# Small products of an attention adapter in 32-column weights, four column groups side by side

## The chip, the cores and the metric

The kernel runs on one core of a Trainium2 chip. The metric is the device time of one execution in microseconds; of several executions the median is taken. TensorE (PE in the profile) multiplies, VectorE (DVE) and ScalarE (ACT) compute element by element and empty PSUM, GpSimd (POOL) fills constants, scales and issues indirect transfers, and SyncE (SP) issues the other transfers.

## The reference

Everything is float32. x is 2 x 2048 x 640, the context 2 x 128 x 384; its last four rows of each batch belong to an adapter. There are eight heads of 80 columns.

```python
enc, ca = context[:, :124], context[:, 124:]
hs      = mha(x @ Wq, enc @ Wk, enc @ Wv)             # 8 heads
ca_q1   = einsum('btc,th->bch', ca, Wq_ca)            # 384 rows
ca_q1   = ca_q1[:, linspace(0, 383, 2048)]            # each row used several times
ca_hs1  = mha(ca_q1, x, x)
ca_hs2  = mha(ca_hs1 @ Wq, ca @ Wk_ca, ca @ Wv_ca)    # 4 keys per head
out     = (hs + ca_hs2) @ Wout + b_out + x
```

## The kernel before, in words

The adapter's first attention has only 384 different query rows, so it is computed for 384 rows and repeated at the end by an indirect transfer that adds rows to the result. Its second attention has four keys a head. A softmax over four scores needs only differences, so three differences of keys a head are enough. The kernel multiplies these differences with Wq ahead of time and gets, for each batch, a small matrix of 24 columns (8 heads x 3). This matrix and Wq_ca stand side by side in the tiles `wyz` and `wyz4`. Multiplied with a block of x (512 rows) they give `yz`: scores of the adapter on one side, and what its values are contracted with on the other. The values of the adapter are likewise multiplied with Wout ahead of time into `w2_sb`.

The edited parts are these.

- `setup_a2` (L437). It multiplies ca with Wk_ca into the PSUM tile `p2_kca` (in the profile `p_kca`): five chunks of 128 columns of Wk_ca are the weights, three parts of the contraction each, and eight columns of context (2 batches x 4 rows) are the moving side. DVE takes differences and multiplies them with a mask of heads, which gives `blk_kca`, 48 columns. Then for each of five chunks i of Wq's rows, Wq is transposed on TensorE (`pt_wq`, five transposes), copied by ACT (`wqT`), and five products with `blk_kca` as the moving side go to the PSUM tile `pa`. `spread_yz` (L422) writes `pa` into `wyz` and `wyz4`, eight DVE steps.
- `setup_values` (L540). It issues the loads of Wout, multiplies ca with Wv_ca (`pvca`: weights of 8 columns, 320 moving columns, six products), transposes that (`pt_vca`), copies it, masks it on DVE (`blk_vca`, 64 columns), computes the values of the text (`pv`, `vpad`), and multiplies `blk_vca` with Wout (`pw`: weights of 64 columns, 320 moving columns, ten products) into `w2_sb`.
- `contraction` (L776). Near its end it writes the probabilities of the second adapter attention into `p2pad`, 65 columns (64 and one of ones for the bias), transposes it and multiplies it with `w2_sb` (the profile shows these as `po<-w_sb,p2T`).

All products pass through one helper, so they carry line L28; transposes carry L41, DVE's steps L55, most copies L268, and SP's transfers L247.

**What sets the order of the work.** TensorE's instructions stay in the order in which the program writes them. That order is made by a planner. `weave` (L1106) runs a main sequence that yields a number of microseconds at certain points; at each, so many microseconds of filling work are written, by a running estimate `pe.us` of TensorE's time. There are two fills: `own` (setup of keys and values, loads and turnings of x, the yz blocks, in this order) and `text` (the queries of the text, block by block). The fill that has used less time goes first; a part that waits for an earlier one is passed over. `fill.until` forces one part to its end without the other fill. In setup the main sequence is `setup_a2`, then the yz block of x block 0, then `maxima` (L743), which for each x block multiplies six times four row groups into a PSUM tile of four banks (`s`), reduced by DVE in one step (`mx`, 128x2048).

A block of x comes by eight transfers on SP (`x_load`, L675, tile `xi`, one buffer) and is turned by five DVE transposes (`x_turn`, L694, tile `xt`). A turning is written when 24 us of `pe.us` have passed since its load; where no data order forbids it, the order of DVE's instructions is settled when the program is built, from estimated times, so it can differ from the written one. The next load waits until the buffer `xi` is free, and the transfers on SP keep their written order: the loads of Wout stand behind the load of x block 3. PSUM tiles of the setup come from a pool of three (`ps_m`) and one of a single tile (`ps_a`).

Of the kernel before, what the change touches and what calls it, by code (L numbers as in the profile page):

```python
# [8 lines left out]
F32 = mybir.dt.float32  # L9
# [4 lines left out]
P = 128  # L14
HEADS = 8
# [158 lines left out]
def kernel(  # L174
# [114 lines left out]

# [36 lines left out]
    N2 = B * HEADS * T  # L326
    w2_sb = const.tile([N2 + 1, H], F32, name="w2_sb")
    p2pad = const.tile([P, NCC, N2 + 1], F32, name="p2pad")
# [66 lines left out]
    caT = sp.tile([P, NCC, B * T], F32, name="caT")  # L395
    wqcaT = sp.tile([P, NCH, T], F32, name="wqcaT")

    def setup_first():

        for cc in range(NCC):  # L400
            pt = mm_tile(f"pt_ctx_{cc}")
            for b in range(B):
                transpose(
                    pt[:, b * NTOK : (b + 1) * NTOK], ctx_sb[:, b, cc * P : (cc + 1) * P], ident
                )
            evacuate(ctxT[:, cc, :, :].rearrange("p b t -> p (b t)"), pt[:, : B * NTOK])
        dve.tensor_copy(
            caT.rearrange("p c (b t) -> p c b t", b=B), ctxT[:, :, :, NK:]
        )
# [26 lines left out]

    def setup_a2():  # L437

        mask = sp.tile([P, NCH, HEADS], F32, tag="mask", name="mask")
        nc.gpsimd.memset(mask, 0.0)  # L440
        for c in range(4):
            nc.gpsimd.tensor_copy(mask[:, c, 2 * c : 2 * c + 2], side)
        nc.gpsimd.tensor_copy(mask[:, 4, :].rearrange("p (g j) -> p g j", j=2)[:, :, 1], quarter)
        kca_of = columns(w_c["kca"], sp.tile([P, NCC, P], F32, tag="w4", name="kca4"))
        p2 = mm_tile("p2_kca")
        for c in range(NCH):
            for cc in range(NCC):
                matmul(
                    p2[:, c * B * T : (c + 1) * B * T],
                    kca_of(cc, c),  # L450
                    caT[:, cc, :],
                    start=(cc == 0),
                    stop=(cc == NCC - 1),
                )
        yield 4.0
        load_w("vca", Wv_ca)
        flat = sp.tile([P, NCH, B, T], F32, name="flat_kca")
        dve.tensor_copy(flat.rearrange("p c b t -> p (c b t)"), p2[:, : NCH * B * T])
        diff = sp.tile([P, NCH, B, T1], F32, name="diff_kca")
        dve.tensor_tensor(  # L460
            diff, flat[:, :, :, 1:], flat[:, :, :, :1].to_broadcast([P, NCH, B, T1]), ALU.subtract
        )
        blk = sp.tile([P, NCH, B, HEADS, T1], F32, tag="blk", name="blk_kca")
        for b in range(B):
            dve.tensor_tensor(
                blk[:, :, b, :, :],
                diff[:, :, b, :].unsqueeze(2).to_broadcast([P, NCH, HEADS, T1]),
                mask.unsqueeze(3).to_broadcast([P, NCH, HEADS, T1]),
                ALU.mult,
            )  # L470

        pa = mm_tile("pa2", ps_a)
        for i in range(NCH):
            wqT = sp.tile([P, NCH, P], F32, tag="wqT", name=f"wqT_{i}", bufs=2)
            for c0, c1 in ((0, 4), (4, NCH)):
                pt = mm_tile(f"pt_wq_{i}_{c0}")
                for c in range(c0, c1):
                    transpose(
                        pt[:, (c - c0) * P : (c - c0 + 1) * P],
                        wq_of(i, c),  # L480
                        ident,
                    )
                evacuate(
                    wqT[:, c0:c1, :].rearrange("p c s -> p (c s)"), pt[:, : (c1 - c0) * P]
                )
            yield 1.5
            for c in range(NCH):
                matmul(
                    pa[:, i * B * Y : (i + 1) * B * Y],
                    wqT[:, c, :],  # L490
                    blk[:, c, :, :, :].rearrange("p b h t -> p (b h t)"),
                    start=(c == 0),
                    stop=(c == NCH - 1),
                )
            yield 1.5
        spread_yz(pa[:, : NCH * B * Y].rearrange("p (i b k) -> p i b k", i=NCH, b=B), 0)
# [43 lines left out]
    def setup_values():  # L540
# [10 lines left out]
        vca = sp.tile([B * T, NCH * P], F32, name="vca")  # L551

# [13 lines left out]
        for u in range(2):  # L566
            pv = mm_tile(f"pvca_{u}")
            for cc in range(NCC):
                matmul(
                    pv[: B * T, :HALF],  # L570
                    caT[:, cc, :],
                    w_c["vca"][:, cc, u * HALF : (u + 1) * HALF],
                    start=(cc == 0),
                    stop=(cc == NCC - 1),
                )
            s4 = pv[: B * T, :HALF].rearrange("p (h d) -> p h d", h=4)
            evacuate(
                vca[:, : 4 * P].rearrange("p (h d) -> p h d", d=VH)[:, 4 * u : 4 * u + 4],
                s4[:, :, :VH],
            )  # L580
            evacuate(
                vca[:, 4 * P :].rearrange("p (h d) -> p h d", d=VR)[:, 4 * u : 4 * u + 4],
                s4[:, :, VH:],
            )
            yield
        pt = mm_tile("pt_vca")
        for c in range(NCH):
            transpose(
                pt[:, c * B * T : (c + 1) * B * T], vca[:, c * P : (c + 1) * P],
                ident[: B * T, : B * T],  # L590
            )
        vcaT = sp.tile([P, NCH, B, T], F32, name="vcaT")
        evacuate(vcaT.rearrange("p c b t -> p (c b t)"), pt[:, : NCH * B * T])
        mask = sp.tile([P, NCH, HEADS], F32, tag="mask", name="mask_v")
        nc.gpsimd.memset(mask, 0.0)
        for c in range(4):
            nc.gpsimd.tensor_copy(mask[:, c, 2 * c : 2 * c + 2], side2)
        nc.gpsimd.tensor_copy(mask[:, 4, :], eighth)
        blk = sp.tile([P, NCH, B, HEADS, T], F32, tag="blk", name="blk_vca")
        for b in range(B):  # L600
            dve.tensor_tensor(
                blk[:, :, b, :, :],
                vcaT[:, :, b, :].unsqueeze(2).to_broadcast([P, NCH, HEADS, T]),
                mask.unsqueeze(3).to_broadcast([P, NCH, HEADS, T]),
                ALU.mult,
            )
        yield
        for b in range(B):
            nc.gpsimd.memset(vpad[b], 0.0)
            for u in range(2):  # L610
# [10 lines left out]
                yield  # L621
        for u in range(2):
            pw = mm_tile(f"pw2_{u}")
            for c in range(NCH):
                matmul(
                    pw[:N2, :HALF],
                    blk[:, c, :, :, :].rearrange("p b h t -> p (b h t)"),
                    wout_sb[:, c, u * HALF : (u + 1) * HALF],
                    start=(c == 0), stop=(c == NCH - 1),
                )  # L630
            evacuate(w2_sb[:N2, u * HALF : (u + 1) * HALF], pw[:N2, :HALF])
            yield
# [143 lines left out]
    def contraction(b, sq, gap):  # L776
# [4 lines left out]
        nc.gpsimd.memset(p2pad[:, :, N2:], 1.0)  # L781
# [63 lines left out]
        n2 = b * HEADS * T  # L845
        dve.tensor_tensor(
# [411 lines left out]
```

## Time and profile before

| what | us |
|---|---|
| median of 3 runs | 773.32 |
| lowest, highest | 772.04, 779.84 |
| profiled execution, whole | 769.24 |
| its span in the profile | 767.5 |
| TensorE busy in the span | 740.0 |
| DVE busy | 374.5 |
| first to last of setup_a2's own products (p_kca to pa) | 22.7 to 51.3 |
| values' setup (pvca to pw) | 99.6 to 117.2 |

The span runs from the first to the last instruction of the profiled execution; 1.7 us of its time lie outside. A product of float32 appears as two instructions, called passes here. A group such as `128*32 128x384` has weights of 128 rows and 32 columns and 384 moving columns. The chain of waits is followed back from the last instruction, at each step to what released it. Ends of TensorE's instructions are modelled, so the distance from one group's start to the next one's is the better measure of what it takes.

### The profile page before, as it was taken

How to read it: one execution, taken by the hardware profiler on the slowest of the kernel's cores; microseconds unless marked ns; L12 is line 12 of the kernel's file. 1: busy time of each engine (PE TensorE's matmuls, PEld its weight loads, DVE VectorE, ACT ScalarE, POOL GpSimd, SP SyncE). 2: the span in 40 equal slices, each digit the busy share in tenths (PEclk: the TensorE clock that was granted, in tenths of full speed). 3: DMA queues.
4: the chain of work that ended last, by engine and by line, in shares of the span. 5: the costliest groups of instructions: out<-in, count | busy, mean ns of one | idle time of the engine just before them, and what ended most of it. 6: DMA issues, size and time to landing. Idle time of an engine off the chain costs nothing.

```text
span 767.5 us, 9354 instructions
## 1 busy us (share of the span) xinstructions
PE 740.0 (96%) x3785; PEld 379.0 (49%) x3785; DVE 374.5 (49%) x502; ACT 195.0 (25%) x241; POOL 134.3 (17%) x192
## 2 busy tenths in 40 slices
PE   7989999999998999989999999999999999999997
PEld 4653343343354445555545454444533556556664
DVE  2134753562365345478758586421530626346631
ACT  2212121104344433231111110443534321011100
POOL 7000000000111012217221221010010023432320
PEclk9999999999999999999999999999999999999999
DMA  9705530000476674499997277320920427785873
GB/s 288 164 2 67 77 79 0 1 0 1 140 122 139 149 123 130 134 255 178 261 189 205 53 153 128 115 48 18 185 63 1 152 69 228 159 218 165 220 213 91
DMA packets 146853, 95.63 MB, mean 125 GB/s; under 512 B 118069, under 2 KB 118389, under 8 KB 144762
## 3 DMA queue, kind: packets, MB, share of 16 engines
q1 hardware_dynamic: 141690, 84.44, 44.8%
q0 software_dynamic: 5120, 10.59, 8.0%
q8 instruction: 30, 0.49, 0.3%
q14 instruction: 13, 0.11, 0.1%
HBM read 63.48 MB, written 31.52 MB: 124 GB/s over the span
## 4 chain that ended last, share of the span: by engine, by line
PE 87%; DVE 6%; DMA 2%; ACT 2%; issue 2%; SPq 0%; POOL 0%; DVEq 0%; ACTq 0%; POOLq 0%
PE po L28 22%; PE pq L28 22%; PE s L28 13%; PE sc L28 10%; PE acc L28 6%; PE ph L28 5%; PE pyz L28 3%; DVE m L55 1%; PE pk L28 1%; DVE p L55 1%; ACT ea L807 1%; PE pt_y L41 1%; DVE mx L55 1%; PE pv L28 1%; DMA pT<-kept 1%
## 5 line engine op out<-in xcount | busy, mean ns | idle before, releaser
L28 PE MATMUL po<-wout_sb,hsT 128*128 128x320 f32 x640 | 187.4, 438 | 0.9 <-DVE xo L55 0.6
L28 PEld LDWEIGHTS po<-wout_sb,hsT 128*128 128x128 f32 x640 | 118.3, 190 | 72.0 <-issue 28.2
L55 DVE TENSOR_REDUCE mx<-s 128x4 f32<-128x2048 f32 x48 | 109.9, 2289 | 83.1 <-PE s L28 83.0
L28 PE MATMUL pq<-xt,wq_sb 128*128 128x512 f32 x320 | 150.2, 605 | 0.0
L807 ACT ACTIVATE ea<-s 128x1536 f32<-128x1536 f32 x64 | 92.7, 1448 | 105.3 <-PE s L28 105.1
L55 DVE TENSOR_TENSOR xo<-xo,po 128x320 f32<-128x320 f32 x64 | 30.9, 483 | 152.7 <-PE po L28 152.7
L962 POOL TENSOR_TENSOR p<-p,r 128x992 f32<-128x992 f32 x32 | 63.6, 2030 | 231.2 <-DVE r L55 231.2
L28 PE MATMUL sc<-kpad,q 128*128 128x248 f32 x384 | 95.4, 385 | 2.2 <-DVE p L55 1.6
L28 PEld LDWEIGHTS pq<-xt,wq_sb 128*128 128x128 f32 x320 | 57.4, 189 | 79.4 <-issue 74.7
L28 PEld LDWEIGHTS sc<-kpad,q 128*128 128x128 f32 x384 | 68.8, 189 | 32.9 <-issue 19.5
L28 PE MATMUL s<-ca,yz 32*128 32x384 f32 x512 | 59.4, 533 | 4.5 <-ACT ea L807 4.1
L268 ACT COPY q<-pq 128x512 f32<-128x512 f32 x30 | 17.6, 585 | 164.2 <-PE pq L28 164.2
L55 DVE TENSOR_REDUCE m<-sc 128x4 f32<-128x496 f32 x64 | 42.2, 662 | 34.0 <-PE sc L28 34.0
L28 PE MATMUL s<-yz,ca 32*128 32x512 f32 x384 | 54.7, 640 | 3.2 <-DVE mx L55 3.2
L1044 POOL DMA_INDIRECT xo<-o,query x25 | 39.2, 1569 | 92.5 <-DVE xo L55 24.1
L28 PE MATMUL acc<-ea,y_sb 128*32 128x384 f32 x512 | 54.6, 498 | 0.0
L28 PE MATMUL ph<-pT,vpad 128*32 128x256 f32 (+1 forms) x512 | 51.1, 387 | 2.1 <-DMA pT<-kept 1.9
L947 ACT ACTIVATE p<-p 128x992 f32<-128x992 f32 x32 | 33.0, 1030 | 74.2 <-DVE p L55 73.9
L55 DVE TENSOR_TENSOR p<-sc,m 128x496 f32<-128x496 f32 x64 | 42.6, 668 | 1.6
L268 ACT COPY hsT<-ph 128x512 f32<-128x512 f32 (+1 forms) x25 | 12.9, 515 | 106.2 <-PE ph L28 106.2
L55 DVE STREAM_TRANSPOSE eb<-p 128x1024 f32<-128x1024 f32 x32 | 38.0, 1221 | 2.2 <-POOL p L962 2.2
L55 DVE TENSOR_REDUCE r<-p 128x8 f32<-128x992 f32 (+1 forms) x34 | 37.9, 1115 | 0.0
(136 smaller groups left out, 435.5 us busy)
## 6 DMA issues: line engine op xcount, KB each, us to landing
kept<-eb SPq DMA_DIRECT2D x16, 1024.0 KB, 4.8
pT<-kept SPq DMA_DIRECT2D x64, 256.0 KB, 5.2
xi<-in_x_dram SPq DMA_DIRECT2D x44, 256.0 KB, 5.9
xo<-in_x_dram SPq DMA_DIRECT2D x32, 320.0 KB, 5.0
out_dram<-xo SPq DMA_DIRECT2D x25, 320.0 KB, 2.6
xi<-in_x_dram SPq DMA_DIRECT2D x44, 64.0 KB, 5.0
early<-xo SPq DMA_DIRECT2D x7, 320.0 KB, 2.2
xe<-early SPq DMA_DIRECT2D x7, 320.0 KB, 5.1
```

What stands on the lines that cost most here:

```text
L28: ins = self.tc.nc.tensor.matmul(out, lhsT, rhs, **kw)
L41: ins = self.tc.nc.tensor.transpose(out, in_, ident)
L55: self.last = getattr(self.tc.nc.vector, name)(*args, **kw).ins
L268: nc.scalar.copy(dst, src)
L807: nc.scalar.activation(e, q4[:, :, :CAD], AF.Exp, scale=SCALE)
L947: nc.scalar.activation(e[:, :, :NK], e[:, :, :NK], AF.Exp, scale=SCALE)
L962: nc.gpsimd.tensor_tensor(et, et, r.unsqueeze(2).to_broadcast([P, HEADS, NK]), ALU.mult)
L1044: nc.gpsimd.indirect_dma_start(out=t, out_offset=None, in_=o2_of[b], in_offset=bass.IndirectOffsetOnAxis(ap=query[:, st : st + 1], axis=0) ...
```

## The change

Four things are turned round.

- **ca with Wk_ca and Wv_ca** (`by_groups`): the rows of context are now the weights (32 columns, of which 6 or 8 are used; the differences of keys are taken beforehand, in `cadT`), and the columns of Wk_ca or Wv_ca move, 160 at a time. Four pairs of heads go to the four groups of 32 partitions of one PSUM tile. Twelve products take the place of 15 (keys) and 6 (values).
- **The turned form** (`groups_turned`): one transpose of 128 columns, and four small products with the identity for the remaining 32 columns of each pair of heads.
- **With Wq and Wout** (`by_blocks`): the masked blocks `blk` are the weights, 32 columns per pair of heads in four column groups, and then one product with all 128 columns for the chunk of remaining columns. Wq's transposes and the rows of Wout move (128 and 320 columns). With Wq the result is turned, so it is copied to `a2`, transposed five times and spread by eight DVE steps (`spread_chunks`). All five `wqT` are now kept until the end and multiplied in one go.
- **The layout of w2_sb and p2pad**: four groups of 32 instead of 64 columns in a row, so the last contraction has 113 rows instead of 65, and `p2pad` is written by two DVE steps instead of one.

The yields of `setup_a2` change with it: before 4.0 and ten of 1.5, now 2.0 and seven of 1.5. The small matrices of zeros are filled by POOL at the start.

```diff
-    N2 = B * HEADS * T
+    N2 = 3 * G + 2 * B * T
...
-    p2pad = const.tile([P, NCC, N2 + 1], F32, name="p2pad")
+    p2pad = const.tile([P, NCC, P], F32, name="p2pad")
...
+    for t in (caT, cadT, blk["k"], blk["v"]):
+        nc.gpsimd.memset(t, 0.0)
...
+    def by_groups(name, rows, w):
+        pg = mm_tile(name)
+        for cc in range(NCC):
+            for g in range(4):
+                matmul(
+                    pg[G * g : G * (g + 1), :D2], rows[:, cc, :], w[:, cc, D2 * g : D2 * (g + 1)],
+                    start=(cc == 0), stop=(cc == NCC - 1), skip_group_check=True,
+                )
+        return pg
+
+    def groups_turned(name, t, n):
+        pt = mm_tile(name)
+        transpose(pt[:, :P], t[:, :P], ident)
+        for g in range(4):
+            matmul(
+                pt[R * g : R * (g + 1), P : P + n], t[:, P:], ident[:, G * g : G * g + n],
+                start=True, stop=True, skip_group_check=True,
+            )
+        return pt[:, :P].rearrange("p (c k) -> p c k", c=4), pt[:, P : P + n]
+
+    def by_blocks(name, *products):
+        for to, rhs, first in products:
+            for c in range(4):
+                matmul(
+                    to[G * c : G * (c + 1)], blk[name][:, 0, c, :], rhs(c),
+                    start=first, stop=False, skip_group_check=True,
+                )
+        for to, rhs, _ in products:
+            matmul(
+                to, blk[name][:, 1].rearrange("p g k -> p (g k)"), rhs(4),
+                start=False, stop=True, skip_group_check=True,
+            )
...
     def setup_a2():
+        pg = by_groups("p2_kca", cadT, w_c["kca"])
+        k2 = sp.tile([P, D2], F32, name="k2")
+        evacuate(k2, pg[:, :D2])
+        yield 2.0
         load_w("vca", Wv_ca)
...
             yield 1.5
-            for c in range(NCH):
-                matmul(
-                    pa[:, i * B * Y : (i + 1) * B * Y],
-                    wqT[:, c, :],
-                    blk[:, c, :, :, :].rearrange("p b h t -> p (b h t)"),
...
+            if i == 0:
+                most, rest = groups_turned("pt_k2", k2, B * T1)
...
+                yield 1.5
+        a2 = sp.tile([P, NCH * P], F32, name="a2")
+        pa = [mm_tile("pa2_0", ps_a), mm_tile("pa2_1")]
+        by_blocks(
+            "k",
+            *[(pa[i // 4][:, i % 4 * P : (i % 4 + 1) * P], lambda c, t=wqT[i]: t[:, c], i % 4 == 0)
+              for i in range(NCH)],
+        )
+        nc.scalar.copy(a2[:, : 4 * P], pa[0])
+        dve.tensor_copy(a2[:, 4 * P :], pa[1][:, :P])
+        yield 1.5
+        for c0, c1 in ((0, 4), (4, NCH)):
+            pt = mm_tile(f"pt_a2_{c0}")
+            for c in range(c0, c1):
+                transpose(pt[:, (c - c0) * P : (c - c0 + 1) * P], a2[:, c * P : (c + 1) * P], ident)
+            for b in range(B):
+                n = 2 * T1
+                w = pt[:, : (c1 - c0) * P].rearrange("p (c g k) -> p c g k", g=4, k=G)
+                spread_chunks(w[:, :, :, n * b : n * (b + 1)], b, c0)
...
+        pg = by_groups("pvca", caT, w_c["vca"])[:, :D2].rearrange("p (j d) -> p j d", j=2)
...
+        most, rest = groups_turned("pt_vca", vca, B * T)
...
+        yield
         for u in range(2):
-            pw = mm_tile(f"pw2_{u}")
...
+            cols = slice(u * HALF, (u + 1) * HALF)
+            pw = mm_tile(f"pw2_{u}")[:, :HALF]
+            by_blocks("v", (pw, lambda c: wout_sb[:, c, cols], True))
+            evacuate(w2_sb[:N2, cols], pw[:N2])
+        yield
...
-        dve.tensor_tensor(
-            p2pad[:, :, n2 : n2 + HEADS * T].rearrange("p a (h t) -> p a h t", t=T), p2.rearrange("p (a h) t -> p a h t", a=NCC),
...
+        for j in range(2):
+            k0 = 2 * T * b + T * j
+            dve.tensor_tensor(
+                p2pad[:, :, : 4 * G].rearrange("p a (g k) -> p a g k", g=4)[:, :, :, k0 : k0 + T],
...
```

## The prediction

> **What bounds the kernel now.** I read the page first (busy shares, slices, chain of waits), then the chain in order of time and the windows for the first 170 us, where all the edited code but one step runs, then the timeline for the nearest rows of the new operations.
>
> ```profile
> PE 740.0 (96%) x3785; PEld 379.0 (49%) x3785; DVE 374.5 (49%) x502; ACT 195.0 (25%) x241; POOL 134.3 (17%) x192
> PE 87%; DVE 6%; DMA 2%; ACT 2%; issue 2%; SPq 0%; POOL 0%; DVEq 0%; ACTq 0%; POOLq 0%
> ```
> These are the page's busy line and the chain's shares: TensorE is the path, so an instruction taken from it is worth its own pitch, provided that nothing else then comes late. The chain in order of time shows what the edited products cost:
>
> ```profile
> 22.70 3.25 PE p_kca L28 x30
> ...
> 49.38 0.59 ACT wqT L268
> ...
> 50.02 1.33 PE pa L28 x10
> ...
> 52.22 4.55 PE pyz L28 x12
> ...
> 72.38 2.93 PE pyz L28 x12
> ...
> 99.59 3.34 PE pvca L28 x12
> ...
> 103.72 1.81 PE pv L28 x6
> ...
> 111.65 5.26 PE pw L28 x19
> ```
> Columns are start, length, engine and tile. A float32 product appears as two passes (x30 for 15 products). The first pyz takes 4.55 us, the next, equal one 2.93. The windows say why, in the column before the last two (granted clock, 1.00 and 0.80):
>
> ```profile
> 22.70:51.34 28.64, 27.38 (x155) 20.77 (x154) 6.20 (x17) 5.43 (x13) 0.81 (x6) 1.00 0.39 96
> 51.34:59.80 8.46, 6.82 (x29) 2.38 (x29) 4.58 (x13) 2.43 (x4) 0.00 (x0) 0.80 0.30 47
> ```
>
> **Price of a 32-column pass.** The timeline has two such groups, four column groups side by side, each with the start of its successor:
>
> ```profile
> 177.00 0.85 PE L28 MATMUL acc<-ea,y_sb 128*32 128x384 f32 x8
> 177.79 1.98 PE L28 MATMUL pq<-xt,wq_sb 128*128 128x512 f32 x4
> 304.51 1.07 PE L28 MATMUL ph<-pT,vpad 128*32 128x256 f32 x16
> 305.51 1.52 PE L28 MATMUL sc<-kpad,q 128*128 128x248 f32 x6
> ```
> Ten full-width po passes of 320 columns take 2.69 us in the chain, 0.84 ns a column. acc needs 0.79 us for two sets of four passes: 2 x 384 x 0.84 = 0.645, leaving 0.14. ph needs 1.00 for four sets: 4 x 256 x 0.84 = 0.86, leaving 0.14. So four passes cost as much as one, plus about 0.14 us a block. [...]
>
> **Setup of the adapter's keys (setup_a2).** Removed: p_kca 3.25; pa, four times 1.05 and once 1.33, 5.5. Together 8.8. Its stalls: 0.6 before the last pa (waits for ACT's wqT), 0.9 before pyz (waits for DVE's wyz), 1.6 for the half clock (4.55 - 2.93).
> Added on TensorE:
> - by_groups, 12 products of 160 columns = 6 sets. Lower end 6 x 160 x 0.84 = 0.8; upper end, if a set can't be shorter than the shortest seen (ph's 0.215), 1.3; with 0.14 I take 1.2.
> - groups_turned: one transpose 0.11 (pt rows) and eight tiny passes, between 0.2 (side by side) and 0.7 (one by one at pt_vca's 0.09); with 0.14, 0.6.
> - by_blocks: 20 narrow products of 128 columns = 10 sets, 1.1 to 2.15, and five full ones, 10 passes x 0.11 = 1.1: 2.8 with the block.
> - five transposes of a2, 0.55.
>
> Sum 5.15 against 8.8. The copies of a2 (ACT 0.59 by the 128x512 wqT row, DVE about 0.2) lie behind two pq products (1.7 us) that the planner's 1.5 lets in; uncovered they would cost 0.7. The spread's eight DVE steps lie behind the last pq product (0.86) but for 0.3. With the fill shorter, pk steps follow each other with only 0.55 us of transposes between, while DVE needs 2 x 0.43 to empty one and three PSUM buffers turn: twice 0.4, against 0.34 today, so +0.5. I expect full clock at pyz, as wide products stand in each stretch ahead of it.
>
> **Setup of the values.** Removed: 99.59 to 103.72 (pvca, its transposes and their wait for ACT) 4.1, and pw 5.3. Added: by_groups 1.2, groups_turned 0.6, by_blocks twice 2 sets x 320 x 0.84 + 2 passes x 0.27 + 0.14 = 2 x 1.2 = 2.4. Here a wait is added: the four DVE steps that build blk stand between the turned groups and by_blocks, and the planner is then forcing this stage alone to reach the next yz block, so no pq fills in. Four steps at 0.23 to 0.28 (pitches of the wyz and blk_vca rows) and the way through PSUM: 1.25. All of TensorE's queue stands behind it, as it keeps program order.
>
> **Elsewhere.** p2pad is written by two DVE steps instead of one. In the second contraction TensorE already waits 0.58 for it, and the one step took 0.91 there (0.25 in the first): +0.3, at most 0.9. The transposes stay at 128 moving columns and the products on w2 at 320; 113 rows instead of 65 in the contraction cost nothing: four passes of 320 columns take 1.24 us with 65 rows (po on w_sb) as with 128 (po on wout_sb). The four memsets on POOL (wyz's 128x256 took 0.30, s2f's 128x96 0.17: 0.9 in all) go ahead of 22 us, and POOL is idle for 12 us from 14.8 on; caT's copy on DVE may wait for them, 1 us at most, and is needed at 22.7. No DMA is added; SP's order stays.
>
> **Sum.** Removed 18.2 of products and 3.1 of stalls. Added 5.15 + 4.2 = 9.35 of products (ends about 8 and 11.3) and waits of 0.5 + 0.3 + 1.25 + 0.3 = 2.35. Saved 9.6 us: of the profiled execution's 769.24 (span 767.5) that makes 759.6; of the median 773.32, four above it, 763.7. I say 764. From 170 us on the instruction stream on TensorE is the same, and it is the path there, so I take the lead as kept.
>
> **Rivals.**
> A: the turning of x block 1 falls behind a reduction. Today DVE does those five transposes at 52.88, in its idle time before the first maximum:
>
> ```profile
> 52.88 3.07 DVE L55 STREAM_TRANSPOSE xt<-xi 128x512 f32<-128x512 f32 x5
> 59.94 2.29 DVE L55 TENSOR_REDUCE mx<-s 128x4 f32<-128x2048 f32 x1 [3.99 <-PE s L28]
> ```
> They stand after that maximum in the program and were placed ahead of it by an order fixed at build time. Their data had long landed, and DVE's idle time before 51 was not used, so the order reckoned with a later landing. With TensorE some 8 us ahead, the first scores come at about 50 us, and the maximum (2.3), perhaps the last kpad steps (1.6), go first; the queries of block 1 then wait 4 to 5 us. [...] Saved then 9.6 - 5 - 0.8 = 3.8, so 769.5. For it: the placement of the second block's turn, split around a maximum. Against: the order depends on reckoned times that no row shows.
> B: the column groups don't run side by side for these short passes. Then by_groups costs 24 x 0.134 = 3.2 twice, the k blocks 4.4 + 1.1, the v blocks 5.3, with the rest 19 us against 18.2 removed: 773. The acc and ph rows speak against it.
> C, slower: the weights for pw come late. The Wout loads are queued on SP behind the load of x block 3, which waits until block 2 is turned (84.7); they end at about 105. With the products ahead of pw shorter by 3 us, the slack of 6 shrinks to 3. If block 2's turn slips behind further maxima (3.8 us a step), by_blocks waits with all of TensorE behind it. Together with A's 5.8 this turns the sign once Wout is over 3.8 us late, that is, after a slip of 7, two steps: 775 to 783.
>
> **How the numbers follow.** The main case 50%, A 32%, B 8%, C 10%. A measurement of this kernel tells about 1% from no change (its runs span 772 to 780). 1% is 7.7 us: the main case (763.7, 3 to either side) passes it three times in four, A one in six, so faster 0.43, slower by over 1% only in C's far half, 0.06. The range: 759 (all costs at their lower ends, 1.4 less, and some of the noise) to 773 (A and B).
>
> **What would show it.** In the profile after: p_kca and pvca as 128*32 groups of about 1 us; by_blocks on pa and pw 2.8 and twice 1.2; pyz the first time at 2.9 with clock 1.00; the first maximum starting near 51 us instead of 59.9, and pq right behind the first scores (main) or after an idle stretch of 4 us ended by DVE's xt (A); a wait of about 1.2 before pw on DVE's blk; sc of the first tile near 158 instead of 168. The prediction is wrong if the 32-column passes have a floor above 0.05 us each, if the clock falls elsewhere, or if the order on DVE shifts after 170 us and gives the lead back.

## The result and the profile after

The changed kernel takes 762.52 us (median of six executions, 759.39 to 765.65) against 774.19 of the kernel before (six, 772.04 to 779.84). The ratio on record is 0.9859 with a 95% interval of 0.9825 to 0.9892 (the quotient of these two medians is 0.985): faster, by more than 1%. Predicted were 764.0 us in a range of 759 to 773. The profiled execution after is 764.96 us (span 763.3). It belongs to the slower half of the six: three took 759.4 to 760.3 us, three 764.7 to 765.7.

The page's busy line and the chain's shares of the kernel after:

```profile
PE 734.3 (96%) x3809; PEld 372.8 (49%) x3809; DVE 374.9 (49%) x506; ACT 195.3 (26%) x240; POOL 133.7 (18%) x184
PE 87%; DVE 6%; DMA 3%; ACT 2%; issue 1%; POOL 0%; SPq 0%; DVEq 0%; ACTq 0%; POOLq 0%
```

TensorE is still the path. The chain of waits in order of time (start, length, engine and tile), after:

```profile
9.08 2.29 DVE x_last L55
...
13.57 14.56 PE pq L28 x30
28.13 0.95 PE p_kca L28 x24
...
45.56 2.54 PE pa L28 x50
...
51.43 3.05 PE pyz L28 x12
...
99.19 0.95 PE pvca L28 x24
...
109.00 2.89 PE pw L28 x20
```

The keys' first products fell from 3.25 to 0.95 us, those of `pvca` from 3.34 to 0.95, `pw` from 5.26 to 2.89, and the first `pyz` from 4.55 to 3.05. But the edited stage starts later: `p_kca` at 28.1 us, where it stood at 22.7 (22.54 by the start of its first pass, which the next table uses). The windows of the same two stretches as before show the clock (the column before the last two) at 1.00 in both:

```profile
28.06:51.43 23.37, 22.03 (x158) 14.33 (x158) 5.35 (x18) 5.89 (x15) 0.00 (x0) 1.00 0.38 101
51.43:59.80 8.37, 7.59 (x37) 3.71 (x38) 5.60 (x10) 2.84 (x5) 0.00 (x0) 1.00 0.46 67
```

Cut into stages by the starts of TensorE's groups, the two profiled executions compare so (us):

| stage | before | after | difference |
|---|---|---|---|
| start to the first p_kca | 22.54 | 28.06 | +5.52 |
| p_kca to the first scores s | 36.11 | 28.31 | -7.80 |
| s to the first sc of the text | 109.33 | 106.48 | -2.85 |
| first sc to the end | 599.57 | 600.41 | +0.84 |
| span | 767.55 | 763.26 | -4.29 |

The cut at the first s does not part equal work. The last group of pk takes 1.40 us (46.22 to 47.62 before, 57.44 to 58.84 after, start to start); it stood ahead of the first scores and now stands behind them. For equal work the two differences are -6.40 and -4.25.

The edited stretch, from p_kca to the first sc, gives 10.65 us, and more than half of it is lost again before that stretch begins. These are the two things that the experiments have to explain. "Stage" below means p_kca to the first sc, 145.44 us before and 134.79 after.

### The profile page after: what moved, and what is told of

Read it like the earlier page. It is cut to its first block, busy times and chain, and to the rows that moved or that the text cites. A ratio compares the mean times of both kernels' runs of the same rounds, so it can differ in the third digit from the quotient of the medians.

```text
span 763.3 us, 9394 instructions
## 1 busy us (share of the span) xinstructions
PE 734.3 (96%) x3809; PEld 372.8 (49%) x3809; DVE 374.9 (49%) x506; ACT 195.3 (26%) x240; POOL 133.7 (18%) x184
## 4 chain that ended last, share of the span: by engine, by line
PE 87%; DVE 6%; DMA 3%; ACT 2%; issue 1%; POOL 0%; SPq 0%; DVEq 0%; ACTq 0%; POOLq 0%
PE po L28 22%; PE pq L28 22%; PE s L28 13%; PE sc L28 10%; PE acc L28 6%; PE ph L28 6%; PE pyz L28 3%; PE pk L28 1%; ACT ea L846 1%; PE pt_y L41 1%; DVE mx L55 1%; DMA pT<-kept 1%; PE pv L28 1%; DVE p L55 1%; DVE m L55 1%
## 5 line engine op out<-in xcount | busy, mean ns | idle before, releaser
L28 PE MATMUL pq<-xt,wq 128*128 128x512 f32 x80 | 38.0, 603 | 0.0
```

Source lines behind the costliest of these rows:

```text
L28: ins = self.tc.nc.tensor.matmul(out, lhsT, rhs, **kw)
```

## Experiments

### Each half alone

The first kernel keeps the keys' edits and has the values as before, the second the reverse (both diffs against the kernel after).

```diff
-        pg = by_groups("pvca", caT, w_c["vca"])[:, :D2].rearrange("p (j d) -> p j d", j=2)
...
+        for u in range(2):
+            pv = mm_tile(f"pvca_{u}")
...
```

```diff
-        pg = by_groups("p2_kca", cadT, w_c["kca"])
...
+        p2 = mm_tile("p2_kca")
...
```

> The keys' products turned round as in the change; the values' products, w2_sb and p2pad as before. My theory (TensorE is the path, each part gives what it takes from it): the stretch from the start of p_kca to the end of the first pk of the last chunk falls from 37.1 us to about 30.9, and the rest is as before: 6 us faster than the kernel before. Rival (the gain is that of the values alone, or the keys' gain is only the half clock at the first pyz that happened to go): about 1.6 us faster, with the stretch at 35.5.

> The values' products, w2_sb and p2pad turned round; the keys' products as before. My theory: the stretch from there to the first sc falls from 108.2 us to about 103.9, the first stretch stays at 37.1 with the half clock at the first pyz (length 4.5), so 4 to 4.5 us faster than the kernel before; together with the keys alone the sum of the change. Rival (the wait on the four DVE steps and the broader contraction give it back): no difference.

Keys alone took 764.84 us (ratio 0.9894, 0.9852 to 0.9935), with a stage of 139.42 us: 6.02 less than before. It is 7.82 less up to the first s and 1.80 more behind it: 1.40 is the group of pk that now stands there, and TensorE waits longer for the maxima. Total, number and longest of these waits, before and then in this kernel:

```profile
PE s L28 <- DVE mx L55: 3.2, 3, 1.4
PE s L28 <- DVE mx L55: 3.7, 4, 1.4
```

The kernel after has the second line too. Values alone took 767.41 (0.9917, 0.9897 to 0.9937). There the stretch that holds the values, s to the first sc, is 104.79 us, 4.54 less; p_kca to s grew by 2.87, for this execution ran 3.41 us from 26.66 and 6.83 from 53.96 at half clock, where the profiled one of before had 3.41 from 51.89. The halves add up: 6.02 + 4.54 = 10.56, against 10.65 for both. The medians lie further under the 774.02 of the kernel before in the same session (9.2 and 6.6 us), but they hold the start and the clock as well; the stages are the measure of the edits.

### Group after group

The 24 passes of each by_groups go out with all contraction parts of one column group before the next group, instead of the four groups in turn. It was to test rival B: what the passes cost when they do not run side by side.

```diff
-        for cc in range(NCC):
-            for g in range(4):
+        for g in range(4):
+            for cc in range(NCC):
                 matmul(
                     pg[G * g : G * (g + 1), :D2], rows[:, cc, :], ...
```

> The change, but by_groups takes the three parts of one column group one after another, and only then the next group; same 12 products each. My theory (four neighbouring products in four column groups run side by side, and products of one group follow each other): p_kca and pvca take about 24 x 0.134 = 3.2 us each instead of 0.95, so 4.5 us slower than the change. Rival (what counts is the 32-column weight, or the queue finds the side-by-side order itself): 0.95 each, no difference to the change.

762.48 us (0.9839, 0.9809 to 0.9869); the stage is 136.55 us, 1.76 more than after, or 0.88 for each by_groups. TensorE's timeline shows the first of them, ahead of pk, at 31.29 - 29.45 = 1.84 us:

```profile
29.45 1.91 PE L28 MATMUL p_kca<-w_kca,cadT 128*32 128x160 f32 x24
31.29 1.56 PE L28 MATMUL pk<-ctxT,w_k 128*128 128x256 f32 x6
```

The single passes explain it. In the kernel after, the four passes of a set start 7 ns apart, and the sets 136 (the first 160). Here passes of one group start 136 ns apart, but the next group's first pass starts about 0.30 us after the first pass of the group ahead, while that one still runs. So TensorE overlapped the groups here, 0.30 us apart, though the program has them one after another, and this order never gave the serial case; the 3.2 us for each group, which rival B and the expectation had, did not appear even here, and the order of the program is worth 0.88 us for each.

### Block 1 turned behind the first maximum

Rival A as an experiment: DVE's order is held so that the five transposes of x block 1 come after the first maximum.

```diff
+            elif behind_max:
+                dve.behind(ins, behind_max.pop())
...
+                if (b, sb, ct, u) == (0, 0, 0, 0):
+                    behind_max.append(dve.last)
```

> The change, with the turning of x block 1 kept behind the first maximum on DVE. This is rival A of the prediction, made to happen. If its price was sized rightly: after the first scores and the last pk, TensorE is idle 4 to 5.5 us until the fourth xt step, 5 to 6 us slower than the change, up to 1.6 more if the clock falls. If the later stretches take it back (the next maxima find a free DVE): under 2 us slower.

766.02 us (0.9904, 0.9880 to 0.9928); the stage is 141.91, 7.12 more. The median is only 3.5 over the kernel after, because half of that one's executions start late; this profiled execution does not (p_kca at 23.39). On DVE the order is the one that rival A described, and TensorE waits for it. First DVE, then TensorE, then the windows around that wait:

```profile
52.98 2.29 DVE L55 TENSOR_REDUCE mx<-s 128x4 f32<-128x2048 f32 x1 [5.76 <-PE s L28]
55.19 1.62 DVE L55 TENSOR_SCALAR kpad<-pk,quarter 128x248 f32<-128x248 f32 x4
56.73 3.07 DVE L55 STREAM_TRANSPOSE xt<-xi 128x512 f32<-128x512 f32 x5
```

```profile
59.35 3.75 PE L28 MATMUL pq<-xt,wq_sb 128*128 128x512 f32 x4 [5.02 <-DVE xt L55]
63.03 1.80 PE L28 MATMUL s<-yz,ca 32*128 32x512 f32 x8
```

```profile
49.00:57.60 8.60, 4.56 (x26) 2.21 (x22) 4.62 (x7) 2.43 (x4) 0.00 (x0) 1.00 0.00 1
57.60:66.00 8.40, 6.65 (x15) 2.36 (x16) 3.21 (x5) 0.00 (x0) 0.00 (x0) 0.59 0.54 80
```

The wait is 5.02 us, and the clock falls to a mean of 0.59 behind it, which stretches four pq passes from 1.72 to 3.75 us. In the kernel after the same transposes stand at 51.80, ahead of the first maximum at 57.65: rival A was priced rightly and did not occur.

### The values' blocks built before the last products of the text's values

The wait for DVE's blk was the one that the prediction had TensorE pay in full. Here the turned groups and the four DVE steps come behind the first `pv` group instead of behind the last.

```diff
                 spread(vpad[b][:NK], pv[:NK, :HALF], u)
                 yield
+                if (b, u) == (0, 0):
+                    most, rest = groups_turned("pt_vca", vca, B * T)
+                    ...
-        most, rest = groups_turned("pt_vca", vca, B * T)
...
```

> The change, with the turned groups of the values and the four DVE steps on blk moved ahead, behind the first pv product group instead of the last. My theory: the wait of 0.84 before pw goes, nothing else moves, 0.8 us less from pvca to the end of pw. Rival (those DVE steps then stand in front of a maximum or a turning and delay it): the next scores wait as long, no gain.

In this kernel and in the seventh below the added loop reuses the name of the outer loop's batch, so that the values of four heads of batch 0 stay zero and those of batch 1 are computed twice; number and shapes of the instructions are unchanged. It took 759.36 us (0.9809, 0.9769 to 0.9850), stage 134.07, 0.72 less than after. TensorE's timeline of the kernel after, then of this one:

```profile
107.91 0.25 PE L28 MATMUL pt_vca<-ident,vca 128*32 128x8 f32 x8
109.00 2.89 PE L28 MATMUL pw<-wout_sb,blk_v 128*32 128x320 f32 x20 [0.84 <-DVE blk_v L55]
```

```profile
100.44 5.11 PE L28 MATMUL pv<-w_v,ctxT 128*128 128x320 f32 x18
105.49 2.89 PE L28 MATMUL pw<-wout_sb,blk_v 128*32 128x320 f32 x20
```

The wait of 0.84 is gone and the pw group is the same 2.89: the wait cost about what it showed. The median lies further under that of the kernel after (3.2 us) than this edit explains; the rest is start and clock.

### What makes the start late

Two causes stand beside each other in the kernel after: the clock is full only from 16.52 us (7.51 before), and DVE's copies of x end only at 11.4 us (8.7 before). The first pair of kernels (called the sixth and the eighth below) puts seven products of zeros at the start of the kernel after and of the kernel before, to raise the clock early.

```diff
+    warm = y_sb[:, 0, :4, :].rearrange("p h k -> p (h k)")
+    dve.memset(warm, 0.0)
+    warmed = mm_tile("warmed")
+    for _ in range(7):
+        matmul(warmed[:, :P], warm, warm, start=True, stop=True)
```

> The change, with seven products of zeros (128x128, results unused) on TensorE before the first transposes, in the time in which it waits for the context. Theory (the executions of one kernel differ by up to 5 us because TensorE's clock is raised sooner or later after the start): the clock is full before the first query product in every execution, p_kca starts at 23.5 or sooner, the spread of the runs shrinks to 2 us and the median is about 759.5. Rival (the late starts come from x rows that land late): still two groups of times, 3 us apart or more, the median gains 1 to 2 us at most.

> The kernel before with the same products of zeros ahead. If the clock at the start is what spreads the runs, it gains as much as the change gains by them, about 2 to 3 us on the median, and the difference to the change with them is 9.6 us by the profile's stages. If late x rows are, no more than 1 to 2 us.

With them the kernel after has full clock from 7.34 us, and p_kca starts at 25.18: 2.88 us earlier, but still 2.64 later than before. So about half of the 5.52 is the clock, and half is not. The time does not show the gain: 762.05 (0.9836, 0.9797 to 0.9874), within 0.5 of the plain change, with the same spread (758.61 to 764.57). A stretch of 3.41 us at half clock takes 0.5 x 3.41 / 763 = 0.0022 from the mean granted clock, which leaves out the start (the profiled execution after has 0.998 with one stretch, though its clock is full only from 16.52); three of these five executions have 0.994 or 0.995, two to three stretches, where five of the six of the plain change have 0.998, one stretch. The kernel before gains 0.3% (769.90; 0.9967, 0.9936 to 0.9998). For the other half, first DVE's and then POOL's timeline of the kernel after:

```profile
7.66 0.23 DVE L55 COPY x_last<-xz 128x128 f32<-128x128 f32 x1 [2.13 <-DMA xz<-in_x_dram]
9.08 2.34 DVE L55 COPY x_last<-xz 128x128 f32<-128x128 f32 x2 [1.19 <-DMA xz<-in_x_dram]
11.34 0.14 DVE L55 TENSOR_REDUCE ones<-ones 128x1 f32<-128x4 f32 x1
```

```profile
9.12 0.33 POOL L404 MEMSET blk_k<- 128x256 f32 x1
9.37 0.33 POOL L404 MEMSET blk_v<- 128x256 f32 x1
9.62 0.44 POOL L566 MEMSET steps<- 128x384 f32 x1
9.98 0.62 POOL L570 MEMSET first<- 128x1 f32 x16
10.51 0.76 POOL L632 MEMSET vpad<- 128x768 f32 x1
```

The copy at 7.66 takes 0.23 us. The two that start at 9.08 and 9.88, when their rows have landed, end at 11.35 and 11.42, as POOL's row of memsets does. Five traces have this row and copies that start between 9.08 and 10.12; all of these end between 11.35 and 11.47, and none that starts ahead of 9.0 takes over 0.55 us. Of the row only blk_k and blk_v are the change's own, 0.5 us from 9.12 to 9.62. The memset of steps stood ahead of the transfers' issue in the kernel before, and those of vpad stood at 13.01, behind the affine selects; the new memsets of caT and cadT now take the time at 4.52.

```profile
4.59 0.41 POOL L504 MEMSET steps<- 128x384 f32 x1
```

The two kernels with zero products isolate the hold: both have full clock before 8 us. In the sixth, with the row of memsets, the last copy of x is held. In the eighth, the kernel before, it starts 0.05 earlier and is not held: POOL still issues transfers, from 7.78 on, and its next step, a copy of a tiny mask, comes at 9.37, when the copy has ended. The lines are DVE's of the sixth, DVE's of the eighth and POOL's of the eighth:

```profile
9.10 2.30 DVE L55 COPY x_last<-xz 128x128 f32<-128x128 f32 x1 [0.57 <-DMA xz<-in_x_dram]
```

```profile
9.05 0.23 DVE L55 COPY x_last<-xz 128x128 f32<-128x128 f32 x1 [0.56 <-DMA xz<-in_x_dram]
```

```profile
9.37 0.54 POOL L448 COPY mask<-side 128x2 f32<-128x2 f32 x4
```

2.30 against 0.23 is 2.07 us, and p_kca starts at 25.18 and 23.14, 2.04 apart. So of the 5.52 in the plain change some 2.9 is the clock, 2.1 the hold, and the rest rows that land later (the last copy starts at 9.88, against 8.44 in the first profile of before).

The test takes the memsets away from that time: DVE writes the same zeros and ones, in the first four microseconds, in which it has nothing to do (its first step in the kernel after starts at 4.60). POOL's remaining steps move up with that.

```diff
-    for t in (caT, cadT, blk["k"], blk["v"]):
-        nc.gpsimd.memset(t, 0.0)
+    for t in (caT, cadT, blk["k"], blk["v"], vpad[0], vpad[1]):
+        dve.memset(t, 0.0)
+    steps = sp.tile([P, NST, STEPS], F32, name="steps")
+    dve.memset(steps, 1.0)
...
-        nc.gpsimd.memset(steps, 1.0)
-            nc.gpsimd.memset(vpad[b], 0.0)
```

> The change with one thing moved: the zeros of caT, cadT, the two blk tiles and both vpad tiles, and the ones of steps, are written by DVE before its first copy of x (it stands idle until 4.5 us), and no longer by POOL at 9.1 to 11.3 us. Theory (POOL's burst of memsets holds DVE's copies of x that start after 9 us): every copy of x takes about 0.23 us wherever it starts, also after 9 us; p_kca starts at 22.5 to 24 us instead of 28.06; the upper group of the change's times (764.7 to 765.7) is gone, and the median falls from 762.5 to about 759.5. Rival (the rows of x land late, and the memsets only stand beside it): a copy that starts after 9 us still ends about 11.3, and the median stays within 1 us of 762.5.

758.79 us (0.9806, 0.9768 to 0.9844), six executions from 757.62 to 760.89. p_kca starts at 22.71; the stage is 134.64. The kernel after has three executions at 759.4 to 760.3 and three at 764.7 to 765.7; here none lies in the upper group. DVE's timeline:

```profile
1.80 1.50 DVE L55 MEMSET vpad<- 128x768 f32 x2
...
8.27 0.23 DVE L55 COPY x_last<-xz 128x128 f32<-128x128 f32 x1 [0.80 <-DMA xz<-in_x_dram]
...
9.96 0.33 DVE L55 TENSOR_SCALAR wyz<-wqcaT,side 128x16 f32<-128x16 f32 x1
```

In this profiled execution the rows had all landed by 8.3 us, so no copy of x met the critical time; the DVE steps that did, on wyz from 9.96 to 11.45, took 0.22 to 0.33. In the seventh kernel, in the next part, with the memsets on POOL, the same wyz steps from 10.23 took up to 1.07 and none ended before 11.3. So the profile shows that the hold is gone for wyz; for the copies of x the sixth and eighth kernels and the times speak. Of the upper group of the kernel after only one execution has a trace, so that the other two started late as well is inferred. Half clock does not part the two groups: five of the six have the same mean clock, 0.998. With the row of memsets on POOL, executions at a mean clock of 0.999 or 1.00 lie far apart: 763.8 to 769.3 for the keys alone, 759.2 to 766.2 for group after group, 757.8 to 763.8 for the early blocks. With the zeros on DVE, those at 1.00 lie between 757.6 and 758.4. Part of the lower median is fewer stretches at half clock: three of these six have none, and all six of the kernel after have at least one.

Last, the kernel before was profiled a second time, since its first profiled execution lies 4 to 5 us under its median.

> The kernel before, unchanged, profiled a second time: its first profiled execution (769.24) lies 4 to 5 us under its own median (773 to 774). If its slower executions also start late, p_kca begins at 25 us or later and the part after the first sc stays at 599.6; if they lose the clock more often, p_kca begins at about 22.5 and one or two more stretches of 3.41 us at half clock stand in the trace, about 2 us each. If it comes out near 769 again, neither is shown. From p_kca to the first sc 145.4 us in each case, plus 2 us for a stretch at half clock that falls inside.

It took 772.2 us: p_kca at 23.67 (1.13 later), the stage 147.12 (1.68 longer) and 599.71 behind it. The extra is a second stretch at half clock, in the window here by the clock of 0.94, where the first profile had 1.00 from 22.70 to 51.34:

```profile
22.00:52.00 30.00, 29.37 (x150) 21.36 (x148) 5.93 (x17) 5.85 (x13) 0.81 (x6) 0.94 0.40 98
```

This is the usual case. Of the 35 executions of the kernel before that are on record with the experiments, two have a mean clock of 0.998, one stretch as in the first profile, and 33 have 0.996 or less, two stretches or more. That they fall in the keys' stage only the profiles show. Against this execution, the kernel with zeros on DVE (757.62 profiled) gains 14.58 us: 0.96 in the start, 12.48 in the stage, 1.14 behind it.

### A version that is faster than both

Three kernels (e7, e9 and e11, called the seventh, ninth and eleventh) put together what helped: blocks early, zero products, and Wq's small transposes in the other pool of PSUM banks, so that the buffers of pk come free sooner. The seventh kernel is that; the ninth is the same with a loop variable of its own, so that both batches' values are complete; the eleventh adds the zeros on DVE.

```diff
-                pt = mm_tile(f"pt_wq_{i}_{c0}")
+                pt = mm_tile(f"pt_wq_{i}_{c0}", ps_a if c0 else None)
```

> The change with the blocks early, the products of zeros ahead, and the transposes of Wq's last chunk in the single PSUM tile that is free then, so that the pk steps find a free buffer. Theory: two waits of 0.5 before pk go, 0.84 before pw, so 1.8 us less than with the products of zeros alone from p_kca to the first sc. Rival (the planner's order leaves the time idle elsewhere, at the wait for yz or the maxima): less than 0.5.

> The change with three edits: the blocks of the values built ahead of pv (now for both contexts), the small transposes of Wq in the other pool of banks, and seven zero products at the start. Expected as the run before it that had the same instructions: p_kca to the first sc 132.2 us, against 134.8 of the change, and a median of 755.5 (754.9 to 759.4, by whether the rows of x land before 9 us).

> The kernel before it with the zeros on DVE as well. Theory of the memset burst: p_kca at 23.0 us in every execution, p_kca to the first sc 132.2, and all times near 755, so that the upper end (759.4) is gone; the ratio to the kernel before about 0.976. Rival (late rows of x): the spread stays 754.9 to 759.4. If DVE's own memsets delay the first copies of x instead, the copy that starts at 5.2 us starts up to 2 us later, and p_kca is no earlier than 24.5.

| kernel | median, lowest to highest | ratio to before | p_kca | stage |
|---|---|---|---|---|
| seventh | 755.50, 754.94 to 759.39 | 0.9768 (0.9732 to 0.9804) | 22.98 | 132.24 |
| ninth | 756.71, 755.08 to 763.07 | 0.9763 (0.9714 to 0.9811) | 26.91 | 132.25 |
| eleventh | 756.76, 755.34 to 759.59 | 0.9785 (0.9745 to 0.9824) | 22.91 | 132.21 |

The stage is 132.2 in all three, 2.55 less than after. For the seventh 1.8 was expected. The difference lies ahead of the first scores, 1.83 instead of 1.0: by their starts, three groups of pk stood 0.40, 0.77 and 0.77 us behind the last transpose ahead of them in the kernel after, and stand 0.11 behind it here. The idle time that the profile gives for them, 0.5 twice, is less, because ends on TensorE are modelled. The ninth's profiled execution is a late one (760.99), and its DVE timeline shows the hold once more:

```profile
9.15 2.28 DVE L55 COPY x_last<-xz 128x128 f32<-128x128 f32 x1 [0.25 <-DMA xz<-in_x_dram]
9.29 2.13 DVE L55 TENSOR_REDUCE ones<-ones 128x1 f32<-128x4 f32 x1
9.36 2.07 DVE L55 COPY caT<-ctxT 128x24 f32<-128x24 f32 x1
```

A row of x that lands at 9.15 instead of 8.79 (the seventh kernel) stands, with a stretch at half clock from 13.22, for 3.9 us at p_kca. With the zeros on DVE the highest time falls from 763.07 to 759.59, but the median does not move (756.71, 756.76), against the expectation that the upper end would be gone and all times near 755. The clocks on record show what is left. In the eleventh the three executions at 1.00 took 755.3 to 756.4, one at 0.998 took 757.1 and two at 0.995 took 759.1 and 759.6. In the ninth those at 1.00 took 755.1 and 755.7, and the highest had 0.991, four stretches. So the fall of the highest time is at least in part the clock, and the zeros on DVE are not shown to gain here. Any of these kernels is some 6 us, 0.8%, faster than the kernel after.

## Why the prediction was right, and where it was not

**The bound.** That TensorE is the path and that an instruction taken from it is worth its pitch held: the stage fell by what was cut.

**The price of a 32-column pass.** By the acc and ph rows, 0.84 ns a column for four passes and 0.14 us a block. Sets of 160 columns come every 136 ns, as 160 x 0.84 = 134 says. Six sets are 0.81, the group took 0.95: 0.14 for the block, as forecast. The upper end, a floor of 0.215 a set, is out. But 0.14 is not the whole price. The first full-width pass behind 32-column passes took 0.10 more until the second one started: 320 ns instead of 216 for pk behind p_kca, 533 instead of 429 for pq behind acc in the kernel before. This falls on the next group, where the acc and ph rows don't show it. by_blocks has its full-width passes inside and pays it itself: by its starts it took 2.45 for the keys against 20 x 128 x 0.84 = 2.15 by columns, and 1.41 against 1.08 for each half of pw. That is 0.30 and 0.34, not 0.14.

**The products.** All by starts. Keys: 0.95 + 0.38 (groups turned, 33.53 to 33.91) + 2.45 + 0.54 = 4.3, forecast 5.15. Values: 0.95 + 0.38 (taken from the keys, where no wait follows) + 2.82 = 4.15, forecast 4.2, where a by_groups and a groups_turned that were too dear and a pw too cheap (2.4) cancel.

**The waits** on TensorE, in the profile of after: 0.21 on wyz (forecast 0.3); 1.0 before pk where it was 0.5 (forecast +0.5); 0.84 on blk_v (1.25); p2pad 0.7 instead of 0.6 (+0.3). Together 1.65 instead of 2.35: what was built from DVE's pitches was on the high side.

**The sum.** Keys 8.8 + 3.1 - 5.15 - 0.8 = 5.95, measured alone 6.02. Values 9.4 - 4.2 - 1.25 = 3.95, measured alone 4.54. Together 9.6 forecast with the 0.3 for p2pad behind the stage, so 9.9 for the stage; measured 10.65. With the measured products and waits the sum would give 11.3 (18.2 + 3.1 - 4.3 - 4.15 - 1.55). Of the 0.65 too much, some 0.5 is the longer wait for the maxima and 0.2 the two first passes behind 32-column groups; the sum had neither. The agreement of 5.95 with 6.02 for the keys is thus in part errors that cancel.

**The memsets: the step that failed.** "caT's copy on DVE may wait for them, 1 us at most, and is needed at 22.7." The memsets were costed by their own length and by the tile that they write. What counted was who else was on DVE at that moment: the copies of x, which start everything. And what held them was not the 0.9 us of the four new memsets but a row of 2.2 us, in which older memsets stand beside two of the new ones. One or two copies wait up to 2.3 us; pq starts at 13.57 instead of 9.63, runs 1.5 us longer for a clock that is full only from 16.52 (ahead of that its passes come 0.85 us apart, behind it 0.43), and p_kca comes 5.5 us late, of which the sixth and eighth kernels give 2.9 to the clock and 2.1 to the hold. It was not in the sum, nor in a rival. The view for it was there: POOL's timeline of before has the transfers' issue up to 9.4 us, and anything queued behind that falls where the last rows of x land.

**The clock.** pyz at full clock was right; the first profile shows 1.6 us for it. The reason given, wide products ahead, was the author's assumption; no run tests it. And a stretch at half clock turned up at 228.15 in the profile of after, where a measured wait of 1.79 for ACT's ea lies ahead of it. It costs 1.6 us: the groups from one acc to the next take 4.74 (228.03 to 232.77), and 3.10 with the zeros on DVE (222.61 to 225.71). The kernel before has its stretches in the keys' stage, one in the first profile and two in the second, and its usual execution has two or more. That was not known: the sum stood on an execution that was better than most.

**From 170 us on.** The lead is kept: 600.41 against 599.57 from the first sc, of which 1.6 is the clock; the kernels without that stretch have 598.3 to 598.6, 1.0 to 1.3 less than before. This gain lies at one place and was not forecast: before, sc at 335.65 waits 1.65 for DVE's p; after, the same group, at 330.90, waits 0.69 for ACT's hsT. The eighth kernel, the kernel before with zero products, does not have the wait either, so it does not come from the products turned round.

**Rivals.** A did not occur, and cost what was said when made to (5.0 of waiting). No run shows the 0.8 that its sum has for the clock: behind the wait four pq passes took 3.75 us instead of 1.72, which is 2.0. B is out: even in the worse order the groups overlap (1.84 us for `p_kca`, where the rival has 3.2). C did not occur: no wait before pw is for Wout.

So the mechanism in the stage held, but that the number 764 came within 1.5 of the median of 762.5 is in part luck. The two profiled executions differ by 4.3 us, not by the 9.6 forecast, for one starts late. The medians differ by 11.7, for two reasons that the forecast did not have and that work against each other: half of the executions after start some 5 us late, and a usual execution of the kernel before has more half clock to lose than the one profiled. Without the late start it is 758.8, as the kernel with zeros on DVE shows: under the range of 759 to 773, by a little.

## What to carry to other kernels

Products with few columns on the weights' side gained here by column groups side by side (`p_kca` 0.95 us instead of 3.25, `pw` 2.89 instead of 5.26): these runs price them at the moving columns of one of four, 0.84 ns each, plus about 0.25 us for a block between full-width products: 0.14 in its own length and 0.10 on the first full-width pass behind it. A fill or memset that is moved is to be placed on the engine's timeline, and then the other engine's steps at that same moment are to be read, not only its own consumers; what DVE copies for the very first products is what must not meet it (2.30 us for a copy beside POOL's memsets, 0.23 without them). Profile the kernel before twice when its profiled execution is far from its median, and read the mean granted clock of every execution before a difference of medians is put down to an edit.

## What the runs showed of the hardware

**Memsets on POOL hold DVE's copies.** Beside the row of memsets a copy took 2.30 us in the sixth kernel, and 0.23 without it in the eighth. A held copy is not let in between two memsets: though a 128x256 memset takes 0.33 us, the copies that start at 9.08 and 9.88 in the kernel after end at 11.35 and 11.42, when the row's last memset (10.51 to 11.27) is through. So they wait up to 2.3 us, to the end of the row. Not every step is held: wqcaT, copied out of PSUM at 10.01 in the seventh kernel in the middle of the same memsets, took 0.18 us, and the wyz steps behind it 1.07:

```profile
10.01 0.18 DVE L55 COPY wqcaT<-pt_wqca 128x20 f32<-128x20 f32 x1 [0.76 <-PE pt_wqca L41]
10.23 1.07 DVE L55 TENSOR_SCALAR wyz<-wqcaT,side 128x16 f32<-128x16 f32 x1
```

POOL's affine selects, which follow the memsets, do not hold those steps (0.23 to 0.25 us each, from 12.46 to 13.21 in the ninth kernel).

**Half clock falls on a grid in these profiles.** The stretch of the kernel before and that of the kernel after each last 3.413 us. They start 44.37 us (7.51 to 51.89) and 211.63 us (16.52 to 228.15) after the first full clock, 13.0 and 62.0 times that length; in the second profile of before it is 5.0 and 13.0 times. TensorE's idle time ahead of a stretch does not tell the cases apart. In the 3.41 us ahead of the stretch at 228.15 TensorE was busy for 1.61, as the kernel after shows:

```profile
224.74:228.15 3.41, 1.61 (x16) 0.66 (x18) 1.86 (x3) 2.37 (x2) 0.00 (x0) 1.00 0.74 247
228.15:231.56 3.41, 3.41 (x25) 1.36 (x23) 0.33 (x1) 1.45 (x1) 0.00 (x0) 0.50 0.00 0
```

The kernel with zeros on DVE has the same wait (1.80 us), with 1.64 us of busy time in 3.42 (219.97 to 223.39), and keeps the full clock: its mean is 1.000. At the other end, in the second profile of before, the stretch at 27.36 follows 3.41 us in which TensorE is recorded as busy all the time; they hold `p_kca`, whose products move eight columns each:

```profile
23.95:27.36 3.41, 3.41 (x31) 3.38 (x31) 0.24 (x1) 0.51 (x1) 0.00 (x0) 1.00 0.80 126
27.36:30.77 3.41, 3.41 (x8) 2.11 (x7) 1.76 (x7) 0.00 (x0) 0.81 (x6) 0.50 0.83 142
```

So recorded busy time does not decide in these traces. What does decide stays open.
